# Layer 1's feed-forward: 69-column outputs for every expert, the tokens' norm on ScalarE, and a new order of the pieces

## The chip, the core and the metric

The kernel runs on one core of one Trainium2 chip. A core has TensorE (matrix multiplies; PE in the profile, its weight loads PEld), VectorE (DVE), ScalarE (ACT), GpSimd (POOL) and SyncE (SP, which only issues DMAs). Each engine works through its own list of instructions in order; semaphores tie the lists together. Matmuls write to PSUM, which this kernel uses as eight banks of 128x512 fp32. The metric is the device time of one execution in microseconds. All matrices here are fp32.

## The reference

A vision tower: 32 images of 256x256 become 256 tokens of 256 values each. Two layers follow, each with an attention and a feed-forward part. The change touches only the feed-forward part of layer 1, called stage e in the kernel:

```python
sx = jnp.einsum('bsh,ndh->bnsd', x, hl_w) + hl_b[None, :, None, :]      # 4 heads of 64
q = jnp.einsum('bnsd,neod->bneso', sx, wq)                              # 4 experts per head
k = jnp.einsum('bnsd,nod->bnso', sx, wk)
v = jnp.einsum('bnsd,nod->bnso', sx, wv)
scores = jnp.einsum('bnesd,bntd->bnest', q, k) * d ** 0.5 + causal
att = jax.nn.softmax(scores, axis=-1)
out = jnp.einsum('bnest,bntd->bnesd', att, v)                           # and laid side by side
gs = jax.nn.softmax(jnp.einsum('bnsf,nef->bnse', out, gate_w) + gate_b[None, :, None, :], axis=-1)
mixed = jnp.einsum('bnsed,bnse->bnsd', out.reshape(b, nh, s, ne, d), gs)
hn = layernorm(mixed + resid, ln_g, ln_b)                               # then fc1, relu, fc2, norm,
                                                                        # and a gate over the heads
```

Its input x is the layer norm of the tokens.

## The kernel before

Stages run one after the other: tokenizer, layer 0, layer 1's attention (stage d), and stage e from 1264 us to the end. In stage e the work of an image is cut into 59 pieces (`PIECES`), such as `(scores, 2)` or `(post, 7)`. Nothing is left to a scheduler there: `ROUND` lists pairs (back, piece), and round r does each piece for image r - back, so that nine images are in flight, from the norm of the tokens of one (back -3) to the last addition of another (back 5). When the last image's `(scores, 5)` has been issued, the rest follows a list of its own, `END`. The order of these lists is the order of each engine's instructions.

The pieces of an image, with the engine that does them:

- `tokens` normalizes the image's tokens (VectorE, line 174), `turn` transposes them on TensorE (line 750), `turned` copies them out of PSUM (ScalarE, line 1034), `heads` and `heads_out` make the heads `sx` (line 1059), of which a DMA makes a copy `sw` with the two halves of the partitions exchanged.
- `experts` multiplies `sx` with `A` (queries of all experts folded with the keys), `experts_out` copies to `g`. `head_values` multiplies with `WV`, and `head_values_out` adds `ones_row` on the way to `ev` (VectorE, line 1101).
- `scores` multiplies `sx`/`sw` with `g`, part 2 for the later keys alone. `exponentials` is ScalarE (line 1126, to `et`), and `later_keys` sets what lies above the diagonal to zero on GpSimd (line 1136).
- `outputs` multiplies `et` with columns of `ev`. For expert e these are five columns of its own (four that give the gate's logits and a one that gives the softmax's denominator) and the 64 values. As `ev` is 84 wide, [own 0, own 1, 64 values, own 2, own 3], experts 1 and 2 take 69 neighbouring columns, and experts 0 and 3 take 74, with five that nobody reads. ScalarE copies the 286 columns of all four to `eo` (line 1153).
- `post` 0 to 2 make the gate and weight the experts (VectorE, and GpSimd's multiply, line 1215), 3 adds them up, 15 and 4 square and sum, 5 scales (`er`), 6 transposes, 60 copies (`fxT`), 7 is fc1 on TensorE, 70 its relu (`hx`) and the DMAs that lay fxT and hx side by side (`both`), 8 is fc2, 80 adds (`ey`), 9 and 10 square and sum, 11 scales (`enorm`) and makes the last gate, 12, 120 and 13 transpose twice, 14 adds the tokens and stores.

TensorE runs the matmuls in three forms. Where lhsT has 128 rows and 128 columns it is one array of 128*128 (heads, fc1 and the transposes). `outputs` and fc2 have 64 columns, and two matmuls work side by side (128*64). Experts, head values and scores have 64 rows, and again two work side by side (64*128). All matmuls have line 115, that of the helper `mm`.

A tile from `bank()` is one PSUM bank, taken in turn: each must have been read by its consumer before the eighth allocation after it can be written.

Of the kernel before, what the change touches and what calls it, by code (L numbers as in the profile page):

```python
# [33 lines left out]
F32 = mybir.dt.float32  # L34
AF = mybir.ActivationFunctionType
# [44 lines left out]
def vit_tower(tc, a, out):  # L80
# [89 lines left out]
    def normed(x, b, pair):  # L170

        st, rs, i = at(pair, b)
        for c in range(NC):
            nc.vector.tensor_scalar(
                x[:, c, :], H[b][:, c, :], st[:, i, c, 0:1], rs[:, i * NC + c : i * NC + c + 1],
                ALU.subtract, ALU.mult,
            )
# [371 lines left out]

    EC = NE + 1  # L550
    VC = NE * EC + HD
    TAKE = ((0, 2 * EC + HD), (EC, EC + HD), (2 * EC, EC + HD), (2 * EC, 2 * EC + HD))
    OC = sum(w for _, w in TAKE)

    starts = [sum(w for _, w in TAKE[:e]) for e in range(NE)]
    OWN = [starts[e] + (0, EC, 2 * EC + HD, 3 * EC + HD)[e] - TAKE[e][0] for e in range(NE)]
    MIX = [starts[e] + 2 * EC - TAKE[e][0] for e in range(NE)]

# [63 lines left out]
    def prepare():  # L622
# [13 lines left out]
        for o in (NE, EC + NE, 2 * EC + HD + NE, 3 * EC + HD + NE):  # L636
            nc.gpsimd.memset(ones_row[:, o : o + 1], 1.0)
# [38 lines left out]
        for hp in range(2):  # L676
            for k, o in enumerate((0, 2 * EC + HD)):
                w = WV[:, hp, o : o + 2 * EC].rearrange("p (e x) -> p e x", e=2)
                nc.gpsimd.memset(w[:, :, NE:], 0.0)
                nc.vector.tensor_copy(  # L680
                    w[:, :, 0:NE],
                    pv[:, hp * 16 + k * 8 : hp * 16 + k * 8 + 8].rearrange("p (e x) -> p e x", e=2),
                )
# [27 lines left out]
        for hp in range(2):  # L711
            nc.vector.tensor_copy(WV[:, hp, 2 * EC : 2 * EC + HD], wv_i[:, hp, :])
# [39 lines left out]

    def normed_e(pool, b):
        x = pool.tile([P, NC, D], F32, name="ex")
        normed(x, b, st_e)
        return x

    def features(pool, x):
        xT = pool.tile([P, 2, N], F32, name="exT")
        nc.scalar.copy(xT.rearrange("p k n -> p (k n)"), feature_major(x))  # L760
        return xT
# [250 lines left out]
    with (  # L1012
# [13 lines left out]
        def tokens(b, im):  # L1026
            im.x = normed_e(p1, b)
# [70 lines left out]
        def head_values_out(b, im):  # L1098
            im.v = p2.tile([P, NC, NH, VC], F32, name="ev")
            for h, p in enumerate(im.pv):  # L1100
                nc.vector.tensor_tensor(
                    im.v.rearrange("p c (k h) x -> p (c k) h x", h=2)[:, :, h, :],
                    p[:, 0 : 2 * NC * VC].rearrange("p (g x) -> p g x", x=VC),
                    over(ones_row, [P, 2 * NC, VC], 1), ALU.add,
                )

# [34 lines left out]
        def outputs(b, im, j):  # L1141
            if j == 0:
                im.o = p2.tile([P, NC * NH, 360], F32, name="eo")
            n, c = ((0, 0), (1, 0), (0, 1), (1, 1), (2, 0), (3, 0), (2, 1), (3, 1))[j]
            p, o = bank(), 0
            for e in range(NE):
                x, w = TAKE[e]
                for m in range(c + 1):
                    t = im.t[n, e, True] if m else im.t[n, e, False][:, c * P : (c + 1) * P]
                    for q in (slice(0, HD), slice(HD, P)):  # L1150
                        mm(p[q, o : o + w], t[:, q], im.v[:, m, n, x : x + w], m == 0, m == c)
                o += w
            nc.scalar.copy(im.o[:, c * NH + n, 0:OC], p[:, 0:OC])  # L1153

# [32 lines left out]
        def expert_pair(im, k, at, w):  # L1187

            x, step = at[2 * k], at[2 * k + 1] - at[2 * k]
            return im.o[:, :, x : x + 2 * step].rearrange("p g (e x) -> p g e x", e=2)[:, :, :, 0:w]  # L1190

        def post(b, im, i):
# [102 lines left out]
            if i == 14:  # L1295
                softmax_rest(im.gate, NC)

                y = p1.tile([P, NC, D], F32, name="ex" if b > B - 6 and b % 2 else "fout")
# [16 lines left out]
            (tokens,), (turn,), (turned,), (heads,), (heads_out,), (experts, 0), (head_values,), (experts_out, 0),  # L1315
            (experts, 1), (experts_out, 1), (head_values_out,), (scores, 0), (scores, 1), (exponentials, 0),
            (exponentials, 1), (heads_zero,), (later_keys, 0), (scores, 2), (scores, 3), (scores, 4), (scores, 5),
            (exponentials, 2), (exponentials, 3), (exponentials, 4), (later_keys, 1), (exponentials, 5),
            (later_keys, 2), (later_keys, 3), (outputs, 0), (outputs, 1), (outputs, 2), (outputs, 3),
            (later_keys, 4), (outputs, 4), (outputs, 5), (later_keys, 5), (outputs, 6), (outputs, 7), (post, 0),  # L1320
            (post, 1), (post, 2), (post, 3), (post, 15), (post, 4), (post, 5), (post, 6), (post, 60), (post, 16),
            (post, 7), (post, 70), (post, 8), (post, 80), (post, 9), (post, 10), (post, 11), (post, 12), (post, 120),
# [3 lines left out]
            (1, 39), (0, 24), (0, 25), (-3, 0), (-1, 13), (4, 54), (3, 48), (4, 55), (0, 26), (0, 27), (3, 49),  # L1326
            (-1, 14), (2, 44), (2, 45), (5, 57), (1, 40), (5, 58), (-2, 3), (2, 46), (-1, 15), (-3, 1), (4, 56),
            (-2, 4), (0, 28), (0, 29), (-3, 2), (0, 30), (0, 31), (3, 50), (3, 51), (1, 41), (0, 32), (0, 33),
            (0, 34), (0, 35), (3, 52), (0, 36), (3, 53), (0, 37), (-2, 5), (-2, 6), (-1, 16), (-2, 7), (0, 38),
            (-2, 8), (-2, 9), (-1, 17), (-1, 18), (-2, 10), (1, 42), (-1, 19), (-1, 20), (2, 47), (-1, 21), (1, 43),  # L1330
            (-1, 22), (-1, 23), (-2, 11), (-2, 12),
        )
        END = (
            (3, 47), (0, 21), (0, 22), (2, 43), (5, 57), (5, 58), (0, 23), (4, 54), (2, 44), (3, 48), (3, 49),
            (0, 24), (1, 39), (0, 25), (2, 45), (2, 46), (0, 28), (0, 29), (1, 40), (0, 26), (1, 41), (2, 47),
            (0, 30), (0, 27), (0, 32), (0, 31), (0, 33), (0, 34), (1, 42), (0, 35), (0, 36), (3, 50), (1, 43),
            (3, 51), (0, 37), (3, 52), (2, 48), (2, 49), (0, 38), (0, 39), (1, 44), (1, 45), (1, 46), (4, 55),
            (0, 40), (3, 53), (4, 56), (0, 41), (3, 54), (4, 57), (2, 50), (1, 47), (2, 51), (1, 48), (1, 49),
            (0, 42), (0, 43), (4, 58), (0, 44), (3, 55), (2, 52), (2, 53), (0, 45), (3, 56), (3, 57), (3, 58),
            (0, 46), (1, 50), (0, 48), (1, 51), (0, 47), (1, 52), (0, 49), (2, 54), (2, 55), (2, 56), (2, 57),  # L1340
            (1, 53), (0, 50), (1, 54), (2, 58), (0, 51), (0, 52), (1, 55), (0, 53), (1, 56), (1, 57), (1, 58),
# [412 lines left out]
```

## Time and profile before

| | us |
|---|---|
| Median of 3 runs | 1949.14 (1946.91 to 1950.96) |
| The profiled execution | 1953.11 |
| Its span, first to last instruction | 1951.4 |
| PE busy | 1908.1 |
| DVE busy | 1209.3 |
| POOL busy | 877.5 |
| ACT busy | 821.0 |

The busy times are those of the whole program. Of stage e, 1400 to 1870 us are steady rounds of nine images; the time before that fills the pipeline, and from 1870 us on it drains. The profile's start times are those at which an instruction began on its engine. Since matmuls overlap, the distance between two starts says what one costs, rather than its length.

### The profile page before, as it was taken

Reading aid. Unit: us, or ns where it says so; the run is one execution under the profiler, and the core shown is the slowest. Engines: PE = TensorE matmul, PEld = TensorE weight load, DVE = VectorE, ACT = ScalarE, POOL = GpSimd, SP = SyncE. Lnnn points to the kernel's source line nnn. Section 1 sums busy time; section 2 is a strip of 40 time slices with the busy share of each in tenths; the row PEclk is TensorE's granted clock in tenths of the full one; section 3 lists DMA queues with packets and bytes.
Section 4 is the critical chain, followed back from the end, with each engine's and each line's share of the span. In section 5 each row is a group of like instructions: output and inputs, shape, how many; then the busy total and the mean of one; then the engine's idle time right before and its main releaser. Section 6 shows DMA issues by size and latency. Waiting matters only on the chain.

```text
span 1951.4 us, 37903 instructions
## 1 busy us (share of the span) xinstructions
PE 1908.1 (98%) x15108; PEld 1370.5 (70%) x15108; DVE 1209.3 (62%) x3225; ACT 821.0 (42%) x1549; POOL 877.5 (45%) x1072
## 2 busy tenths in 40 slices
PE   9999999999999999999989999999999999999994
PEld 7887676767676767676545555577888888888873
DVE  2334456565656574434365655545788888888886
ACT  0001222121212122212434444367878787878762
POOL 1224224343424252433443343336767676767672
PEclk9999999999999999999999999999999999999996
DMA  8540000000000042221000000011222222222212
GB/s 289 161 148 15 1 17 30 19 22 11 22 12 22 33 140 57 81 62 52 17 11 1 1 1 1 1 23 29 52 55 56 56 54 58 53 60 51 62 51 61
DMA packets 69671, 95.03 MB, mean 49 GB/s; under 512 B 8561, under 2 KB 51057, under 8 KB 69105
## 3 DMA queue, kind: packets, MB, share of 16 engines
q1 hardware_dynamic: 62768, 74.98, 13.4%
q0 software_dynamic: 6144, 16.79, 2.8%
q8 instruction: 121, 1.98, 0.4%
q10 hardware_dynamic: 576, 0.79, 0.1%
q14 instruction: 62, 0.50, 0.1%
HBM read 46.38 MB, written 20.97 MB: 35 GB/s over the span
## 4 chain that ended last, share of the span: by engine, by line
PE 95%; DVE 2%; POOL 1%; DMA 1%; ACT 0%; issue 0%; SPq 0%; ACTq 0%; DVEq 0%
PE bank L115 90%; PE bank L750 2%; PE bank L188 1%; PE bank L1294 1%; DMA patch<-in_patches_dram 0%; POOL hv L1167 0%; PE bank L229 0%; PE bank L482 0%; POOL et L1136 0%; DVE six L123 0%; DMA both<-hx 0%; POOL eo L1215 0%; DVE enorm L1273 0%; DVE ranges L1228 0%; DVE h L827 0%
## 5 line engine op out<-in xcount | busy, mean ns | idle before, releaser
L1136 POOL TENSOR_SCALAR_AFFINE_SELECT et<-et 128x256 f32<-128x256 f32 (+1 forms) x384 | 200.2, 553 | 19.4 <-ACT et L1126 18.8
L115 PE MATMUL bank<-ev,et 128*64 128x74 f32 (+1 forms) x6144 | 205.7, 227 | 1.9 <-POOL et L1136 1.9
L115 PEld LDWEIGHTS bank<-ev,et 128*64 128x64 f32 x6144 | 197.6, 138 | 8.0 <-issue 5.2
L1126 ACT ACTIVATE et<-bank 128x512 f32<-128x512 f32 x384 | 201.0, 660 | 0.0
L115 PE MATMUL bank<-tokW,patch 128*128 128x256 f32 x768 | 169.1, 383 | 2.7 <-DMA patch<-in_patches_dram 2.7
L115 PE MATMUL bank<-g,sx 64*128 64x512 f32 (+1 forms) x512 | 170.7, 483 | 0.0
L115 PE MATMUL bank<-g,sw 64*128 64x512 f32 (+1 forms) x512 | 170.3, 483 | 0.0
L115 PEld LDWEIGHTS bank<-tokW,patch 128*128 128x128 f32 x768 | 147.7, 193 | 24.4 <-issue 3.5
L1153 ACT COPY eo<-bank 128x286 f32<-128x286 f32 x256 | 101.9, 402 | 91.1 <-PE bank L115 78.7
L115 PE MATMUL bank<-bxT,w_wuv 128*128 128x512 f32 x300 | 131.4, 592 | 0.0
L115 PEld LDWEIGHTS bank<-g,sw 64*128 64x128 f32 x512 | 95.7, 187 | 33.0 <-issue 21.9
L148 POOL TENSOR_SCALAR rs_c<-st_c 128x4 f32<-128x4 f32 x16 | 3.1, 191 | 251.8 <-DVE st_c L124 251.8
L1215 POOL TENSOR_TENSOR eo<-eo,gate 128x1024 f32<-128x1024 f32 x60 | 115.2, 1940 | 1.5 <-DVE gate L1212 1.5
L115 PE MATMUL bank<-wvo,dm 128*128 128x512 f32 x256 | 114.3, 599 | 0.0
L115 PE MATMUL bank<-attn,bv 128*128 128x256 f32 x512 | 113.1, 379 | 0.0
L115 PE MATMUL bank<-w_wo,gT 128*128 128x256 f32 x512 | 113.1, 379 | 0.0
L115 PE MATMUL bank<-w_w,hT 128*128 128x256 f32 x512 | 113.1, 379 | 0.0
L115 PE MATMUL bank<-xsel,w_w 128*128 128x512 f32 x256 | 111.4, 592 | 0.0
L1167 POOL TENSOR_TENSOR hv<-hv,minus_half 128x8 f32<-128x8 f32 x64 | 108.8, 1699 | 5.3
L115 PEld LDWEIGHTS bank<-attn,bv 128*128 128x128 f32 x512 | 97.2, 190 | 19.6 <-issue 6.9
L115 PEld LDWEIGHTS bank<-g,sx 64*128 64x128 f32 x512 | 95.7, 187 | 19.4 <-issue 14.8
L123 DVE BATCH_NORM_STATS2 six<-h 128x6 f32<-128x256 f32 x256 | 105.6, 412 | 4.4
(268 smaller groups left out, 3845.6 us busy)
## 6 DMA issues: line engine op xcount, KB each, us to landing
patch<-in_patches_dram SPq DMA_DIRECT2D x31, 768.0 KB, 4.6
sw<-sx SPq DMA_DIRECT2D x64, 128.0 KB, 2.7
both<-fxT SPq DMA_DIRECT2D x64, 128.0 KB, 3.2
both<-hx SPq DMA_DIRECT2D x64, 128.0 KB, 2.4
out_dram<-fout SPq DMA_DIRECT2D x29, 256.0 KB, 2.1
cs<-ranked SPq DMA_DIRECT2D x32, 128.0 KB, 2.0
results<-cy SPq DMA_DIRECT2D x32, 128.0 KB, 1.7
w_w<-in_w_dram SPq DMA_DIRECT2D x2, 1024.0 KB
```

The costliest lines, as they stand in the source:

```text
L115: nc.tensor.matmul(o, lhsT, rhs, start=first, stop=last)
L123: nc.vector.bn_stats(six, x)
L148: nc.gpsimd.tensor_scalar(o, var, 1.0, 1e-5, ALU.mult, ALU.add)
L188: nc.tensor.transpose(p[:, o : o + P], x[:, c, k * P : (k + 1) * P], ident)
L750: nc.tensor.transpose(p[:, o : o + P], x[:, c, k * P : (k + 1) * P], ident)
L1126: nc.scalar.activation(t, p, AF.Exp)
L1136: nc.gpsimd.affine_select(out=own, in_=own, pattern=[[0, n_e], [1, P]], compare_op=ALU.is_ge, fill=0.0, base=0, channel_multiplier=-1,)
L1153: nc.scalar.copy(im.o[:, c * NH + n, 0:OC], p[:, 0:OC])
L1167: nc.gpsimd.tensor_tensor(v, v, minus_half, ALU.pow)
L1215: (nc.vector if b > B - 3 else nc.gpsimd).tensor_tensor(im.mix[k], im.mix[k], over(im.gate[:, :, 2 * k : 2 * k + 2], [P, NC * NH, 2, HD], ...
L1294: nc.tensor.transpose(im.po[:, o : o + P], im.fT[:, k, c * P : (c + 1) * P], ident)
```

## The change

1. `ev` becomes 148 wide: [own 0, 64 values, own 1, own 2, 64 values again, own 3]. Every expert's five columns now lie beside a copy of the values, so each takes 69 columns, from 0, 5, 74 and 79, and `eo` is 276 wide instead of 286. `WV` stays 84 wide, in the order own 0, values, own 1, own 2, own 3. `head_values_out` now writes each half of the heads with three VectorE additions (74 columns, 5 and 5) and one ScalarE copy of the 64, so that there are six and two per image instead of two and none.
2. `tokens` moves from VectorE to ScalarE: an activation with scale and bias per token. The bias, minus mean times scale, is one 128x2 operation on VectorE.
3. `PIECES`, `ROUND` and `END` are ordered anew. On TensorE a round was: post 7, 12, 6 and 13, heads, turn; outputs 0 to 3, post 8, outputs 4 to 7; experts 0, head values, experts 1, scores 2 to 5, 0 and 1. It is now: heads, post 12, 13 and 6; outputs 0 to 3, post 8, outputs 4 to 7; turn; experts 0; post 7; scores 2 to 5, head values, experts 1, scores 0 and 1. On GpSimd `later_keys` 4 and 5 now stand ahead of the multiply of post 2, and 1 to 3 behind it, mixed with the powers of post 10 and 4. Image 31's end list moves too: post 0 and 1 of image 30 and fc1 of image 28 stand ahead of the last scores.
4. The last stores of images 27, 29 and 31 use the buffer of `exT` instead of `ex`.

The diff; of the three lists the old lines are left out:

```diff
--- before.py
+++ after.py
@@ -547,14 +547,16 @@
     LOW, HIGH = 1e-28, 1e28
 
 
     EC = NE + 1
+    WC = EC + HD
     VC = NE * EC + HD
-    TAKE = ((0, 2 * EC + HD), (EC, EC + HD), (2 * EC, EC + HD), (2 * EC, 2 * EC + HD))
-    OC = sum(w for _, w in TAKE)
-
-    starts = [sum(w for _, w in TAKE[:e]) for e in range(NE)]
-    OWN = [starts[e] + (0, EC, 2 * EC + HD, 3 * EC + HD)[e] - TAKE[e][0] for e in range(NE)]
-    MIX = [starts[e] + 2 * EC - TAKE[e][0] for e in range(NE)]
+    VU = 2 * (WC + EC)
+    TAKE = (0, EC, WC + EC, WC + 2 * EC)
+    OC = NE * WC
+    OWN = [e * WC + (0, HD)[e % 2] for e in range(NE)]
+    MIX = [e * WC + (EC, 0)[e % 2] for e in range(NE)]
 
     right_e, right_d, passing = ExitStack(), ExitStack(), ExitStack()
     pwe = right_e.enter_context(tc.tile_pool(name="e_w", bufs=1, side="right", reuse_waits="tile"))
@@ -633,7 +635,7 @@
         ones_d = pm.tile([P, P], F32, name="ones_d")
         nc.gpsimd.memset(ones_d, 1.0)
         nc.gpsimd.memset(ones_row, 0.0)
-        for o in (NE, EC + NE, 2 * EC + HD + NE, 3 * EC + HD + NE):
+        for o in (NE, WC + NE, WC + EC + NE, WC + 2 * EC + NE):
             nc.gpsimd.memset(ones_row[:, o : o + 1], 1.0)
         gfg = pm.tile([P, 2, NH], F32, name="gfg")
         nc.vector.tensor_scalar(gfg, fg, col("fn_g"), None, ALU.mult)
@@ -674,13 +676,10 @@
 
         nc.scalar.mul(A.rearrange("p h x -> p (h x)"), pa, math.sqrt(HD))
         for hp in range(2):
-            for k, o in enumerate((0, 2 * EC + HD)):
-                w = WV[:, hp, o : o + 2 * EC].rearrange("p (e x) -> p e x", e=2)
-                nc.gpsimd.memset(w[:, :, NE:], 0.0)
-                nc.vector.tensor_copy(
-                    w[:, :, 0:NE],
-                    pv[:, hp * 16 + k * 8 : hp * 16 + k * 8 + 8].rearrange("p (e x) -> p e x", e=2),
-                )
+            for e, o in enumerate((0, WC, WC + EC, WC + 2 * EC)):
+                w = WV[:, hp, o : o + EC]
+                nc.gpsimd.memset(w[:, NE:], 0.0)
+                nc.vector.tensor_copy(w[:, 0:NE], pv[:, hp * 16 + e * NE : hp * 16 + (e + 1) * NE])
 
         p = bank()
         mm(p[:, 0 : 2 * NH], cen, gfg.rearrange("p k x -> p (k x)"))
@@ -709,7 +708,7 @@
         centred(f2.unsqueeze(1), f2.unsqueeze(1), 1)
         centred(wv_i, wv_i, 2)
         for hp in range(2):
-            nc.vector.tensor_copy(WV[:, hp, 2 * EC : 2 * EC + HD], wv_i[:, hp, :])
+            nc.vector.tensor_copy(WV[:, hp, EC:WC], wv_i[:, hp, :])
 
         yield
         for i in range(2):
@@ -749,16 +748,6 @@
                 o = k * N + c * P
                 nc.tensor.transpose(p[:, o : o + P], x[:, c, k * P : (k + 1) * P], ident)
         return p
-
-    def normed_e(pool, b):
-        x = pool.tile([P, NC, D], F32, name="ex")
-        normed(x, b, st_e)
-        return x
-
-    def features(pool, x):
-        xT = pool.tile([P, 2, N], F32, name="exT")
-        nc.scalar.copy(xT.rearrange("p k n -> p (k n)"), feature_major(x))
-        return xT
 
 
     class Pair:
@@ -1024,7 +1013,15 @@
         halves = [slice(h * HD, (h + 1) * HD) for h in range(2)]
 
         def tokens(b, im):
-            im.x = normed_e(p1, b)
+            im.x = p1.tile([P, NC, D], F32, name="ex")
+            st, rs, i = at(st_e, b)
+            rs = rs[:, i * NC : (i + 1) * NC]
+            less = spool.tile([P, NC], F32, name="e_less")
+            nc.vector.scalar_tensor_tensor(less, st[:, i, :, 0], -1.0, rs, ALU.mult, ALU.mult)
+            for c in range(NC):
+                nc.scalar.activation(
+                    im.x[:, c, :], H[b][:, c, :], AF.Identity, bias=less[:, c : c + 1], scale=rs[:, c : c + 1]
+                )
 
         def turn(b, im):
             im.pt = feature_major(im.x)
@@ -1096,13 +1093,22 @@
                         mm(p[:, o : o + VC], im.sx[s, hp, c * P : (c + 1) * P], WV[s, hp, :])
 
         def head_values_out(b, im):
-            im.v = p2.tile([P, NC, NH, VC], F32, name="ev")
+            im.v = p2.tile([P, NC, NH, VU], F32, name="ev")
             for h, p in enumerate(im.pv):
+                v = im.v.rearrange("p c (k h) x -> p (c k) h x", h=2)[:, :, h, :]
+                p = p[:, 0 : 2 * NC * VC].rearrange("p (g x) -> p g x", x=VC)
+                first = WC + EC
                 nc.vector.tensor_tensor(
-                    im.v.rearrange("p c (k h) x -> p (c k) h x", h=2)[:, :, h, :],
-                    p[:, 0 : 2 * NC * VC].rearrange("p (g x) -> p g x", x=VC),
-                    over(ones_row, [P, 2 * NC, VC], 1), ALU.add,
+                    v[:, :, 0:first], p[:, :, 0:first], over(ones_row[:, 0:first], [P, 2 * NC, first], 1), ALU.add
                 )
+                nc.vector.tensor_tensor(
+                    v[:, :, first : first + EC], p[:, :, first : first + EC],
+                    over(ones_row[:, first : first + EC], [P, 2 * NC, EC], 1), ALU.add,
+                )
+                nc.vector.tensor_tensor(
+                    v[:, :, VU - EC :], p[:, :, first + EC :], over(ones_row[:, first + EC :], [P, 2 * NC, EC], 1), ALU.add
+                )
+                nc.scalar.copy(v[:, :, first + EC : VU - EC], p[:, :, EC:WC])
 
         def scores(b, im, k):
 
@@ -1140,17 +1146,18 @@
 
         def outputs(b, im, j):
             if j == 0:
-                im.o = p2.tile([P, NC * NH, 360], F32, name="eo")
+                im.o = p2.tile([P, NC * NH * OC + MIX[2]], F32, name="eo")
             n, c = ((0, 0), (1, 0), (0, 1), (1, 1), (2, 0), (3, 0), (2, 1), (3, 1))[j]
             p, o = bank(), 0
             for e in range(NE):
-                x, w = TAKE[e]
+                x, w = TAKE[e], WC
                 for m in range(c + 1):
                     t = im.t[n, e, True] if m else im.t[n, e, False][:, c * P : (c + 1) * P]
                     for q in (slice(0, HD), slice(HD, P)):
                         mm(p[q, o : o + w], t[:, q], im.v[:, m, n, x : x + w], m == 0, m == c)
                 o += w
-            nc.scalar.copy(im.o[:, c * NH + n, 0:OC], p[:, 0:OC])
+            o = (c * NH + n) * OC
+            nc.scalar.copy(im.o[:, o : o + OC], p[:, 0:OC])
 
         def in_range(b, first, n):
             return ranges[:, b // 8 % 2, b % 8, first : first + n]
@@ -1187,7 +1194,8 @@
         def expert_pair(im, k, at, w):
 
             x, step = at[2 * k], at[2 * k + 1] - at[2 * k]
-            return im.o[:, :, x : x + 2 * step].rearrange("p g (e x) -> p g e x", e=2)[:, :, :, 0:w]
+            rows = im.o[:, x : x + NC * NH * OC].rearrange("p (g x) -> p g x", x=OC)
+            return rows[:, :, 0 : 2 * step].rearrange("p g (e x) -> p g e x", e=2)[:, :, :, 0:w]
 
         def post(b, im, i):
             if i == 0:
@@ -1295,7 +1303,7 @@
             if i == 14:
                 softmax_rest(im.gate, NC)
 
-                y = p1.tile([P, NC, D], F32, name="ex" if b > B - 6 and b % 2 else "fout")
+                y = p1.tile([P, NC, D], F32, name="exT" if b > B - 6 and b % 2 else "fout")
                 y8 = y.rearrange("p c (n d) -> p (c n) d", d=HD)
                 nc.vector.tensor_tensor(
                     y8, im.po.rearrange("p (g d) -> p g d", d=HD),
@@ -1312,33 +1320,32 @@
 
         images = [Image() for _ in range(B)]
         PIECES = (
...
+            (tokens,), (turn,), (turned,), (heads,), (heads_out,), (experts, 0), (experts_out, 0), (head_values,),
+            (head_values_out,), (experts, 1), (experts_out, 1), (scores, 0), (scores, 1), (exponentials, 0),
+            (exponentials, 1), (later_keys, 0), (later_keys, 1), (scores, 2), (scores, 3), (exponentials, 2),
+            (exponentials, 3), (later_keys, 2), (heads_zero,), (scores, 4), (exponentials, 4), (later_keys, 3),
+            (scores, 5), (exponentials, 5), (later_keys, 4), (later_keys, 5), (outputs, 0), (outputs, 1),
+            (outputs, 2), (outputs, 3), (outputs, 4), (outputs, 5), (outputs, 6), (outputs, 7), (post, 0), (post, 1),
+            (post, 2), (post, 3), (post, 15), (post, 4), (post, 5), (post, 6), (post, 60), (post, 7), (post, 16),
+            (post, 70), (post, 8), (post, 80), (post, 9), (post, 10), (post, 11), (post, 12), (post, 120),
             (post, 13), (post, 14),
         )
         ROUND = (
...
+            (0, 28), (0, 29), (-1, 13), (-2, 3), (2, 44), (4, 54), (4, 55), (-1, 14), (5, 57), (2, 45), (-2, 4),
+            (-1, 15), (0, 30), (4, 56), (1, 40), (2, 46), (0, 31), (-3, 0), (0, 32), (0, 33), (5, 58), (3, 50),
+            (0, 34), (3, 51), (0, 35), (-1, 16), (3, 52), (1, 41), (0, 36), (0, 37), (-3, 1), (-2, 5), (3, 53),
+            (-3, 2), (-2, 6), (2, 47), (1, 42), (-1, 17), (-1, 18), (2, 48), (2, 49), (-1, 19), (-1, 20), (0, 38),
+            (0, 39), (-1, 21), (-1, 22), (-1, 23), (-1, 24), (1, 43), (-1, 25), (-1, 26), (-1, 27), (-2, 7), (-2, 8),
+            (-2, 9), (-2, 10), (-2, 11), (-2, 12),
         )
         END = (
...
+            (0, 28), (0, 27), (0, 30), (5, 57), (5, 58), (1, 40), (2, 44), (0, 31), (0, 32), (2, 45), (2, 46),
+            (3, 50), (4, 54), (1, 41), (1, 42), (0, 29), (2, 47), (0, 33), (2, 48), (2, 49), (1, 43), (0, 34),
+            (4, 55), (4, 56), (3, 51), (3, 52), (3, 53), (1, 44), (0, 35), (0, 36), (0, 37), (0, 38), (0, 39),
+            (1, 45), (1, 46), (2, 50), (0, 40), (0, 41), (1, 47), (1, 49), (1, 48), (0, 42), (0, 43), (3, 54),
+            (2, 51), (4, 57), (0, 44), (0, 45), (2, 52), (1, 50), (3, 55), (2, 53), (4, 58), (1, 51), (0, 46),
+            (0, 47), (1, 52), (1, 53), (3, 56), (0, 49), (3, 57), (2, 54), (2, 55), (2, 56), (2, 57), (3, 58),
+            (0, 48), (1, 54), (0, 50), (1, 55), (2, 58), (0, 51), (0, 52), (0, 53), (1, 56), (1, 57), (1, 58),
             (0, 54), (0, 55), (0, 56), (0, 57), (0, 58),
         )
         LAST = PIECES.index((scores, 5))
```

## The prediction

> **What bounds the kernel now.** First the table of stretches, for the stage that the change touches (from 1264 us on):
>
> ```profile
> core 0: us, PE busy (x) PEld busy (x) DVE busy (x) ACT busy (x) POOL busy (x), PEclk, DMA share, GB/s
> 1500.00:1600.00 100.00, 100.00 (x1588) 81.39 (x1586) 85.25 (x203) 80.05 (x175) 69.23 (x93) 1.00 0.22 55
> 1870.00:1951.40 81.40, 51.04 (x682) 38.36 (x679) 60.42 (x158) 33.74 (x71) 35.06 (x45) 0.77 0.20 54
> ```
>
> TensorE has no idle time in the steady rounds; only the tail from 1870 us, at a lower clock, waits. "Busy" counts overlapped latencies, though, so next I read the starts in TensorE's timeline, one round of the loop (start, length of the group, group):
>
> ```profile
> 1600.79 0.59 PE L115 MATMUL bank<-g,sx 64*128 64x512 f32 x1
> 1601.21 0.59 PE L115 MATMUL bank<-g,sw 64*128 64x512 f32 x1
> 1601.22 0.59 PE L115 MATMUL bank<-g,sx 64*128 64x512 f32 x1
> 1601.74 1.13 PE L115 MATMUL bank<-fxT,w_fc 128*128 128x512 f32 x2
> 1602.70 0.60 PE L750 MATMUL bank<-ident,enorm 128*128 128x128 f32 x4
> ...
> 1605.74 0.60 PE L750 MATMUL bank<-ident,ex 128*128 128x128 f32 x4
> 1606.27 3.20 PE L115 MATMUL bank<-ev,et 128*64 128x74 f32 x96
> 1609.30 1.12 PE L115 MATMUL bank<-W,both 128*64 128x68 f32 x32
> 1610.25 3.15 PE L115 MATMUL bank<-ev,et 128*64 128x74 f32 x96
> 1613.33 1.14 PE L115 MATMUL bank<-sx,A 64*128 64x256 f32 x8
> ...
> 1621.31 1.12 PE L115 MATMUL bank<-fxT,w_fc 128*128 128x512 f32 x2
> ```
>
> The round is 1621.31 - 1601.74 = 19.57 us. The form before each size is rows*columns of the array in use. A pair of 64*128 matmuls of 512 columns takes 0.43 us (1600.79 to 1601.22), but the step to the first 128*128 matmul is 0.52, 0.09 too much, and in single records the second w_fc matmul follows 0.533 us after the first where 512 columns need 0.427: 0.106 more. The same two excesses stand wherever the form changes, always alike: 64*128 to 128*128 0.092+0.106; 128*128 to 128*64 0.096+0.053; 128*64 to 64*128 0.095+0.107; 128*128 to 64*128 (layer 1's attention and the first rounds) 0.095+0.107; 128*64 to 128*128 0.096+0.106. So no semaphore causes them; a change of form costs 0.15 to 0.20 us. A round before has three: 0.55 us.
>
> [...]
>
> **The change part by part.**
>
> ```profile
> L1153 ACT COPY eo<-bank 128x286 f32<-128x286 f32 x144 | 57.3, 398 | 47.8 <-PE bank L115 40.2
> L1059 ACT ACTIVATE sx<-bank,cols 128x256 f32<-128x256 f32 x36 | 17.6, 620 | 0.0
> L1238 ACT ACTIVATE fxT<-bank,cols 128x512 f32<-128x512 f32 x18 | 16.3, 907 | 0.0
> L1101 DVE TENSOR_TENSOR ev<-bank,ones_row 128x336 f32<-128x336 f32 x34 | 15.6, 501 | 4.4 <-PE bank L115 4.4
> L174 DVE TENSOR_SCALAR ex<-h,st_e,rs_e 128x256 f32<-128x256 f32 x36 | 13.1, 406 | 0.0
> 1325.33 3.04 ACT L1126 ACTIVATE et<-bank 128x512 f32<-128x512 f32 x6
> ```
>
> *Outputs all 69 wide.* In single starts sixteen 74-wide matmuls take 0.513 us, sixteen 69-wide 0.480; over all stretches 32.0 and 30.1 ns each. Half of an image's 192 narrow: 96 x 1.9 ns = -0.18 us, on the path. For 31 images before the tail: -5.6 us.
>
> *Places anew, on TensorE.* The order of a round is now heads, three transposes (128*128); outputs and fc2 (128*64); the token transpose `turn` (128*128); experts 0 (64*128); fc1, post 7 (128*128); scores 2 to 5, head values, experts 1, scores 0 and 1 (64*128). Six changes of form instead of three: `turn` and fc1 used to stand in one run of 128*128 and are now islands. Added are one 128*64 to 128*128 (0.135: [...] between 0.10 and 0.20), one 64*128 to 128*128 (0.198) and one 128*128 to 64*128, with the 128*64 to 64*128 replaced by an equal one: +0.53. Round: 19.57 + 0.53 - 0.18 = 19.92. Counted in the program's order up to the last image's scores: 96 changes before (17.6 us at these prices), 182 after (32.9 us): +15.2.
>
> *Norm of tokens on ScalarE.* VectorE loses 2 x 406 ns and gains one 128x2 operation (about 0.17). ScalarE gains two of 256 with two per-partition operands: [...]. Hidden in the steady round under TensorE: `turn` needs them only 3 us later. In the first two rounds nothing hides them: `turn` waits for heads_out and then 1.15 us of norm. Before, sx of image 0 ended at 1278.21 while `turn` began at 1278.00; now about 1279.2: +1.2. A round later it ends at 1286.63, so `turn` at 1287.6 and experts 0.58 behind, against 1286.32: +1.9. Together +3.1.
>
> *Values 148 wide.* VectorE: two operations of 336 become two of 296 and four of 20 (0.46 and about 0.17 each; they start some 0.08 before the predecessor ends): +0.5 us; with the norm about zero. ScalarE: two copies of 256 from PSUM, 0.37 (the 286 row less 30 elements), back to back 0.28. ScalarE's round: before 14.3 us at back-to-back pace (the exponentials 12 x 0.476: six take 3.04), after 14.3 + 0.9 + 0.56 - 0.07 = 15.7 of 19.9.
>
> I walked one round in the new order with these durations, heads at 0: outputs 3.2 to 10.0, `turn` 10.1, experts 10.7, fc1 11.7, scores 2 to 5 from 12.8 to 16.3, head values to 17.15, experts 1 to 18.06, scores 0 and 1 to 19.8. Margins before TensorE would wait (8 banks, each taken 8 allocations later): enorm for post 12 is ready at 0.7, wanted at 1.8; bank of outputs 4 wants VectorE's fout, which the POOL multiply ahead of it holds (as at 1604.09, 1.94 us), at 5.8, wanted 7.1; tokens 6.8, wanted 10.1; bank of scores 0 wants the exponentials of scores 4 at 17.0, wanted 18.06; scores 1 those of scores 5 at 17.95, wanted 18.9. All hidden, with 1 us to spare. POOL's order leaves the selects done well before each output.
>
> *Fill and last full round.* Before, TensorE stood 2.6 us in the outputs at 1332 (the selects sat behind POOL's multiplies), 0.4 at 1328 and 1.35 at 1881: 4.3. The selects now stand ahead of the multiplies: these go, the 3.1 above come: -1.2. fc1 of image 28 is done before the tail: +1.0 there.
>
> *Tail.* Before: last score matmul 1889.73, end 1951.4: 61.7 us, a serial chain over the last image with its neighbours' work ahead of it in each queue (outputs done at +15.4, er x rs +31.3, fc2 +41.2, last enorm +50.1, last add ends +55.5, then 6.2). Walked through the new end order with the tail's own durations (VectorE 0.69 per 512, POOL power 1.65 + 0.2, reshuffle 3.0): TensorE waits from +3 to +7 for image 29's er behind the multiplies of image 30; outputs done +14.8, er x rs +28.0, fc2 +39.3, enorm +47.1, add ends +52.5: 58.7, so -3.0, good to 4 us either way.
>
> Sum: +15.2 - 5.6 + 1.0 - 1.2 - 3.0 = **+6.4 us**. The profiled execution took 1953.11 us, 1.7 of it outside its span of 1951.4; it would have a span of 1957.8. The median of the runs is 1949.14, so 1955.5.
>
> **Rivals.** (A) A wait enters each round: ScalarE. An exponential pair takes 0.95 us where a score pair takes 0.85, so ScalarE falls behind in the scores; hx or the gate's exponential 1 us later than walked makes scores 0 wait one for one. For it: ScalarE rises from 73 to 79%. Against: the margins. At 0.3 us in 28 rounds: +8.4, 1964. (B) Fill and tail win more than walked, 7 us instead of 3 and the 3.1 at the start half hidden: 1950, not to be told from before. (C) Faster: the changes of form cost nothing where a semaphore or a load would have held TensorE anyway. Without the 15.2 the sum is -8.8: 1940. 86 more changes decide it at 8.8/86 = 0.10 us each: below that it is faster. Against: the trace shows 0.15 to 0.20 at each one in steady work, in five kinds. (D) The narrowing does nothing because a 64-column load sets the pace: +12, 1961; against, 69 wide is faster than 74 in each stretch, and 68 (29.6 ns) faster still.
>
> **Numbers.** Forecast with or without D 0.58, A 0.17, B 0.17, C 0.08. Single runs of before spread 4 us, and 0.2% (3.9 us) is about what a measurement of this kernel can tell from no change. Range 1950 to 1966: it leaves out C, the better half of B, and an A of over 0.4 us a round. Slower over 0.2%: most of the forecast and A, 0.74; within 0.2%: 0.18; faster: 0.08.
>
> **What would show it.** Right: a steady round of 19.9 us, [...] 69-wide outputs at 30.1 ns; some 1 us before `turn` in the first two rounds; no bubble near 1332. Wrong: a round under 19.6, a steady wait of TensorE on ScalarE, VectorE or POOL, or a tail off 59 us by over 5.

## The result, and the profile after

The changed kernel takes 1966.03 us (median, 1962.50 to 1969.29) against 1950.05 (1946.91 to 1951.98) for the kernel before, measured beside it: a ratio of 1.0083, 95% interval 1.0056 to 1.0110. It is slower by 16 us; the forecast was 6.4 slower. Repeated later it took 1965.96 and 1967.22 (ratios 1.0082 and 1.0087). The profiled execution took 1969.29 us with a span of 1966.6, 15.2 us over the span before. The remaining 0.8 to 1 us isn't in the span: each execution of the changed kernel takes 2.7 to 3.2 us more than its span from first to last instruction, each of the kernel before 1.6 to 1.8 us.

The table of stretches of the kernel after (columns as before):

```profile
core 0: us, PE busy (x) PEld busy (x) DVE busy (x) ACT busy (x) POOL busy (x), PEclk, DMA share, GB/s
1500.00:1600.00 100.00, 100.00 (x1590) 78.84 (x1586) 82.89 (x213) 86.01 (x192) 71.88 (x91) 1.00 0.23 56
1870.00:1966.60 96.60, 63.76 (x992) 49.33 (x988) 77.07 (x198) 46.31 (x101) 47.29 (x55) 0.86 0.21 54
```

In the steady rounds TensorE still has no idle time, at the full clock (PEclk, the granted share of TensorE's clock, is 1.00). ScalarE rose from 80 to 86 and VectorE fell from 85 to 83: neither is the bound. So what grew there is TensorE's own round. One round in TensorE's timeline after (start, length, group):

```profile
1614.12 0.59 PE L115 MATMUL bank<-g,sx 64*128 64x512 f32 x1
1614.64 1.99 PE L115 MATMUL bank<-exT,w_hl 128*128 128x256 f32 x8
...
1617.35 0.60 PE L749 MATMUL bank<-ident,er 128*128 128x128 f32 x4
1617.88 3.11 PE L115 MATMUL bank<-ev,et 128*64 128x69 f32 x96
1620.81 1.12 PE L115 MATMUL bank<-W,both 128*64 128x68 f32 x32
1621.76 3.06 PE L115 MATMUL bank<-ev,et 128*64 128x69 f32 x96
1624.75 0.66 PE L749 MATMUL bank<-ident,ex 128*128 128x128 f32 x4
1625.34 1.13 PE L115 MATMUL bank<-sx,A 64*128 64x256 f32 x8
1626.40 1.12 PE L115 MATMUL bank<-fxT,w_fc 128*128 128x512 f32 x2
1627.46 0.48 PE L115 MATMUL bank<-g,sx 64*128 64x256 f32 x1
...
1634.58 1.99 PE L115 MATMUL bank<-exT,w_hl 128*128 128x256 f32 x8
```

From heads to heads are 19.94 us, and 19.93 on the mean of 24 rounds. `turn` at 1624.75 and fc1 at 1626.40 each stand alone between groups of another form. The step from turn to experts 0 is 0.59 us where four transposes inside a run of their form take 0.44; experts 0 takes 1.06 instead of the 0.97 of before, and fc1 1.06 instead of 0.96.

The groups of ScalarE and VectorE after, 1400 to 1752 us (busy, mean ns, idle before):

```profile
L1160 ACT COPY eo<-bank 128x276 f32<-128x276 f32 x143 | 54.2, 396 | 26.0 <-PE bank L115 23.6
L1022 ACT ACTIVATE ex<-h,e_less,rs_e 128x256 f32<-128x256 f32 x36 | 20.2, 624 | 0.0
L1111 ACT COPY ev<-bank 128x256 f32<-128x256 f32 x34 | 12.8, 376 | 3.2 <-DVE ev L1108 2.8
...
L1101 DVE TENSOR_TENSOR ev<-bank,ones_row 128x296 f32<-128x296 f32 x35 | 16.1, 461 | 51.7 <-PE bank L115 51.7
L1104 DVE TENSOR_TENSOR ev<-bank,ones_row 128x20 f32<-128x20 f32 x34 | 5.7, 167 | 0.0
L1020 DVE SCALAR_TENSOR_TENSOR e_less<-st_e,rs_e 128x2 f32<-128x2 f32 x17 | 2.6, 153 | 0.0
```

The added operations last about what the prediction took for them: 0.38, 0.46, 0.17 and 0.15 us where 0.37, 0.46, 0.17 and about 0.17 stood. An activation of the norm takes 0.62 us, and the pair 1.09 where my estimate was 1.15.

I cut stage e by the starts of groups on TensorE. "Fill" runs from the first transpose of image 0's tokens to the heads of round 0, the third heads; "end" from the heads of round 29, the last image's, to the start of the last score matmul; "tail" from there to the end of the span. r0, r5 and r29 are the starts of rounds 0, 5 and 29. Times are from the profiles, in us; the last three rows are experiments described below.

| | fill | r0 to r5 | r5 to r29 (one round) | end | tail | stage e |
|---|---|---|---|---|---|---|
| before | 20.3 | 94.4 | 469.7 (19.57) | 31.0 | 62.0 | 677.4 |
| after | 29.3 | 92.3 | 478.3 (19.93) | 32.6 | 60.3 | 692.8 |
| after, 2nd profile | 28.1 | 92.3 | 478.3 (19.93) | 32.6 | 61.6 | 692.8 |
| after, 3rd profile | 28.0 | 92.3 | 478.3 (19.93) | 32.6 | 59.9 | 691.1 |
| tokens first | 21.9 | 92.3 | 478.4 (19.93) | 32.6 | 61.3 | 686.3 |
| three forms, tokens first | 21.9 | 90.6 | 465.4 (19.39) | 31.4 | 63.3 | 672.5 |
| places without wide values | 24.7 | 92.9 | 482.8 (20.12) | 32.9 | 60.7 | 694.0 |

Steady rounds (+8.7) and fill (+7.7 to +9.0) carry the loss. The first rounds in the timeline, before, with line 174 VectorE's norm of the tokens:

```profile
1274.65 0.41 DVE L174 TENSOR_SCALAR ex<-h,st_e,rs_e 128x256 f32<-128x256 f32 x1
...
1278.00 0.61 PE L750 MATMUL bank<-ident,ex 128*128 128x128 f32 x4
1278.54 1.14 PE L115 MATMUL bank<-sx,A 64*128 64x256 f32 x8
```

The same in the timeline after (in brackets: idle time before, and what ended it):

```profile
1276.10 1.66 DVE L944 SCALAR_TENSOR_TENSOR h<-bank,d_rs,h 128x256 f32<-128x256 f32 x4 [1.41 <-POOL d_rs L149]
...
1276.95 1.00 PE L115 MATMUL bank<-w_hl,exT 128*128 128x64 f32 x8
1277.15 0.84 ACT L1056 ACTIVATE sx<-bank,cols 128x256 f32<-128x256 f32 x2 [2.08 <-PE bank L115]
...
1278.54 0.27 DVE L1046 TENSOR_TENSOR res<-bank,rows_e 128x128 f32<-128x128 f32 x1
...
1279.13 0.14 DVE L1020 SCALAR_TENSOR_TENSOR e_less<-st_e,rs_e 128x2 f32<-128x2 f32 x1
...
1279.36 1.09 ACT L1022 ACTIVATE ex<-h,e_less,rs_e 128x256 f32<-128x256 f32 x2 [1.37 <-DVE e_less L1020]
...
1280.02 1.39 PE L749 MATMUL bank<-ident,ex 128*128 128x128 f32 x4 [2.07 <-ACT ex L1022]
1281.34 2.08 PE L115 MATMUL bank<-sx,A 64*128 64x256 f32 x8
```

Two things are to be seen. TensorE stood for 2.07 us before `turn`. ScalarE was done with the heads (`sx`) at 1278.0, and its norm then waited 1.37 us for the tokens' bias `e_less`. That stood late in VectorE's list, behind the attention's last additions `h`, statistics of other tokens and `res` (the residual, from the heads' second matmuls); from 1276.10 to `e_less` VectorE had no idle time. Before, the norm stood early in the round, ahead of those additions, and was done at 1275.5. The second wait, 1.27 us a round later, has another cause: there the bias is in time, and the norm starts right behind an exponentials' table load (1.28), four exponentials and `sx` in ScalarE's own list.

Then, `turn` and experts 0 take about twice their time (2.08 where 1.14 was): the clock went to half rate. In the table of stretches PEclk is 0.52 for these 7 us:

```profile
1280.00:1287.00 7.00, 6.97 (x38) 5.49 (x40) 1.18 (x6) 3.02 (x7) 1.20 (x2) 0.52 0.06 12
```

By its clock record after has two such stretches here, 6.83 us from 1279.8 and 3.41 us from 1293.5 (PEclk 0.50 in both); before has none from 993 us to 1893 (PEclk 1.00).

### The profile page after: what moved, and what is told of

Read it like the earlier page. It is cut to its first block, busy times and chain, and to the rows that moved or that the text cites. A ratio compares the mean times of both kernels' runs of the same rounds, so it can differ in the third digit from the quotient of the medians.

```text
span 1966.6 us, 38148 instructions
## 1 busy us (share of the span) xinstructions
PE 1919.8 (98%) x15108; PEld 1361.9 (69%) x15108; DVE 1206.0 (61%) x3325; ACT 871.2 (44%) x1677; POOL 890.8 (45%) x1076
## 4 chain that ended last, share of the span: by engine, by line
PE 94%; DVE 4%; DMA 1%; ACT 1%; issue 0%; POOL 0%; ACTq 0%; DVEq 0%
PE bank L115 89%; PE bank L749 2%; PE bank L188 1%; PE bank L1302 1%; DMA patch<-in_patches_dram 0%; PE bank L229 0%; PE bank L482 0%; DVE eo L1223 0%; DVE six L123 0%; DVE six L934 0%; DVE fout L1312 0%; DVE h L816 0%; DMA tokW<-in_tokW_dram 0%; DVE fout L1308 0%; DVE enorm L1281 0%
## 5 line engine op out<-in xcount | busy, mean ns | idle before, releaser
L1142 POOL TENSOR_SCALAR_AFFINE_SELECT et<-et 128x256 f32<-128x256 f32 (+1 forms) x384 | 214.5, 591 | 78.1 <-ACT et L1132 77.1
L115 PE MATMUL bank<-ev,et 128*64 128x69 f32 x6144 | 197.2, 223 | 0.0
L115 PEld LDWEIGHTS bank<-ev,et 128*64 128x64 f32 x6144 | 189.7, 136 | 6.3 <-issue 5.7
L115 PE MATMUL bank<-g,sx 64*128 64x512 f32 (+1 forms) x512 | 179.9, 490 | 0.0
L115 PE MATMUL bank<-g,sw 64*128 64x512 f32 (+1 forms) x512 | 178.5, 491 | 0.0
L1160 ACT COPY eo<-bank 128x276 f32<-128x276 f32 x256 | 96.5, 397 | 48.2 <-PE bank L115 43.9
```

The lines of the kernel that those rows point to most:

```text
L115: nc.tensor.matmul(o, lhsT, rhs, start=first, stop=last)
L1142: nc.gpsimd.affine_select(out=own, in_=own, pattern=[[0, n_e], [1, P]], compare_op=ALU.is_ge, fill=0.0, base=0, channel_multiplier=-1,)
L1160: nc.scalar.copy(im.o[:, o : o + OC], p[:, 0:OC])
```

## The experiments

All keep the computation of the kernel whole. The theory after seeing the result: the steady rounds cost what was forecast, and the rest is the fill, waits and clock together. Rivals: the wide values' extra work on VectorE and ScalarE; the norm's engine rather than its place.

**Tokens first.** The changed kernel, with the tokens' norm at the head of the round:

```diff
         ROUND = (
-            (0, 28), (0, 29), (-1, 13), (-2, 3), (2, 44), ...
-            ... (0, 31), (-3, 0), (0, 32), ...
+            (-3, 0), (0, 28), (0, 29), (-1, 13), (-2, 3), (2, 44), ...
+            ... (0, 31), (0, 32), ...
```

> The kernel after, with the piece tokens moved to the head of each round, so that the 128x2 operation stands ahead of the residual's addition on VectorE and the norm ahead of heads_out on ScalarE. If the first rounds lost their 9 us because turn waited for the norm (2.2 us and 1.3 us) [...], both go: heads of image 2 start some 7 us earlier (near 1296 us instead of 1303.2), steady round unchanged at 19.93, time 1959 (9 above before). Rival: the loss sits in the new places of experts and head values, and the norm is innocent: 1966, heads of image 2 still near 1303.

Measured: 1959.88 us (1956.34 to 1964.16), ratio 1.0049 (1.0031 to 1.0067). The fill fell by 7.4 us to 21.9, without half rate (experts 0 take 1.13 us), and the steady round is unchanged. So the place of `tokens` costs about 6 us of the 16. It leaves 1.6 us over before in the fill; in that timeline:

```profile
1285.01 1.13 PE L115 MATMUL bank<-sx,A 64*128 64x256 f32 x8 [1.59 <-ACT sx L1056]
```

Experts 0 of image 1 wait for `sx`, which ScalarE makes after the norm, a table load (1.28) and four exponentials.

**Filler.** The changed kernel, and TensorE does eight 128x128 matmuls that nobody reads while it waits, ahead of `turn` of images 1 and 2:

```diff
         def turn(b, im):
+            if b in (1, 2):
+                p = bank()
+                for _ in range(8):
+                    mm(p[:, 0:128], ident, ident)
             im.pt = feature_major(im.x)
```

> The kernel after, with eight matmuls of 128x128 that nobody reads ahead of turn of images 1 and 2 (1.7 us each at full rate), so that TensorE does work while it waits for the norm. If the waits alone cost the time: no change or up to 0.5 us slower, 1966. If the idle time brings the half-rate clock, and that is most of the loss: no half-rate window between 1270 and 1300 us and some 5 us faster, 1961, with the waits for the norm still there.

Measured: 1963.26 us (1960.82 to 1966.81), ratio 1.0069 (1.0054 to 1.0084). No half rate in the fill (PEclk 1.00 from 1263 to 1300 us), which took 25.4 us, although the norm is as late as ever: `turn` of image 1 starts 3.07 us behind the heads' second matmuls in both kernels, and the filler takes 2.00 of it. It lies between the two expectations, and of the 2.8 us won against the changed kernel some 1.1 lie outside the span, where this kernel takes 1.7 us like the kernel before. The profile has 3.9 us less of fill than the 29.3, but a later experiment has the same waits without half rate and without filler (PEclk 1.00), so this one alone would not have settled it.

**Three forms.** Tokens first, and `turn` and fc1 go back into one run of 128*128 with heads and transposes (fc1 one round later):

```diff
-            (0, 28), (0, 29), (-1, 13), (-2, 3), (2, 44), ... (2, 45), (-2, 4),
-            ... (0, 31), (-3, 0), (0, 32), ... (0, 37), (-3, 1), (-2, 5), (3, 53),
-            (-3, 2), (-2, 6), (2, 47), (1, 42), ... (2, 48), (2, 49), (-1, 19), ...
+            (-3, 0), (0, 28), (0, 29), (-1, 13), (3, 47), (3, 49), (-2, 3), (2, 44), ... (2, 45), (-3, 1), (-2, 4),
+            ... (0, 31), (-3, 2), (0, 32), ... (0, 37), (-2, 5), (3, 53),
+            (-2, 6), (1, 42), ... (2, 48), (-1, 19), ...
         END = (
-            (0, 28), (0, 27), ...
+            (3, 47), (3, 49), (0, 28), (0, 27), ...
```

> As e1, and turn and fc1 (post 7, with post 70) put back into the run of 128*128 matmuls around the heads: three changes of form a round instead of six. If changes of form make the steady round: 19.93 - 0.53 = 19.4 us and, with e1's fill, 1944 (6 under before). Rival: the round of 19.93 comes from ScalarE's or VectorE's added work, which is all still here: 19.9 and 1959.

Measured: 1944.91 us (1943.70 to 1948.47), ratio 0.9970 (0.9959 to 0.9980), faster than both kernels. The round is 19.39 us. Its timeline:

```profile
1599.53 0.59 PE L115 MATMUL bank<-fxT,w_fc 128*128 128x512 f32 x1
1599.96 1.89 PE L115 MATMUL bank<-exT,w_hl 128*128 128x256 f32 x8
1601.69 0.60 PE L749 MATMUL bank<-ident,enorm 128*128 128x128 f32 x4
...
1603.00 0.60 PE L749 MATMUL bank<-ident,ex 128*128 128x128 f32 x4
1603.53 3.11 PE L115 MATMUL bank<-ev,et 128*64 128x69 f32 x96
```

The round has three changes of form (two expectations below call them four). Heads take 1.73 from start to start instead of 1.83, the transposes 0.44, and 19.93 - 19.39 = 0.54 us a round is what three more changes of form cost. Step by step, all of it lies where the form changes: 0.15 us at `turn` (0.135 by my estimate) and 0.09 to 0.11 each at experts 0, fc1, the first scores behind it and heads; every other step of the two rounds is equal. They cost time, whatever the reason for their place. (Of the 15 us won over tokens first, about 1 lies outside the span.)

**Wide values alone.** The kernel before with part 1 (and the buffers of part 4), in the old order and with VectorE's norm.

> The kernel before with part 1 of the change alone: values 148 wide, all outputs 69 columns, three VectorE additions and a ScalarE copy per half; norm on VectorE and the old places. If 1.9 ns for each of 96 matmuls an image is right and the added VectorE and ScalarE work is hidden: round 19.57 - 0.18 = 19.39, time 1944.5 (5.6 under before). Rival (a 64-column weight load sets the pace, or VectorE's four more operations delay others): 19.57 or more, 1950 or more.

Measured: 1961.45 us (1959.91 to 1964.29), ratio 1.0055 (1.0040 to 1.0070). I had expected the narrowing's gain and it is a loss: the round is 19.85 us, where 19.39 was expected and 19.57 was before. The narrowing is there (outputs 2.94 and 2.99 us for 96), but the scores take 5.41 instead of 5.26, and post 12's transposes 0.74 instead of 0.44. In its timeline, with ScalarE and TensorE's weight loads:

```profile
1601.36 0.67 ACT L1104 COPY ev<-bank 128x256 f32<-128x256 f32 x2
...
1602.42 3.07 ACT L1125 ACTIVATE et<-bank 128x512 f32<-128x512 f32 x6
...
1606.15 0.14 PEld L749 LDWEIGHTS bank<-ident,enorm 128*128 128x128 f32 x1 [0.24 <-ACT et L1125]
...
1607.29 0.42 PEld L749 LDWEIGHTS bank<-ident,er 128*128 128x128 f32 x4 [0.35 <-ACT et L1125]
```

The bank that a transpose takes must have been read by the exponentials, and they stand behind the two new copies.

**Wide values, copies on VectorE.** The same, with one line changed:

```diff
-                nc.scalar.copy(v[:, :, first + EC : VU - EC], p[:, :, EC:WC])
+                nc.vector.tensor_copy(v[:, :, first + EC : VU - EC], p[:, :, EC:WC])
```

> The kernel with the wide values alone (part 1 in the old order, round 19.85 us, 1961), but the two copies of the 64 values are on VectorE instead of ScalarE. Theory: it was ScalarE's two copies, which stand ahead of the exponentials in its list, that made TensorE wait in the scores (5.41 instead of 5.26 us) and before the transposes of post 12 (0.75 instead of 0.44 us). Then the scores go back to 5.26, the round to about 19.4 to 19.5, and the time to 1945 to 1948. Rival: VectorE's longer work in head_values_out is what is late (its next consumers wait); then the copies on VectorE make it worse, with a round of 19.9 or more and a time over 1962.

Measured: 1947.42 us (1944.72 to 1950.03), ratio 0.9985 (0.9978 to 0.9993). The scores are back at 5.26, post 12's transposes at 0.44 in most rounds (0.52 on the mean), the fill at 20.3 and the round at 19.47. Its timeline:

```profile
1610.47 3.04 ACT L1125 ACTIVATE et<-bank 128x512 f32<-128x512 f32 x6
...
1615.01 0.60 PE L749 MATMUL bank<-ident,enorm 128*128 128x128 f32 x4
...
1615.44 0.60 PE L749 MATMUL bank<-ident,er 128*128 128x128 f32 x4
```

So ScalarE's two copies, 0.67 us ahead of its exponentials, made the old order wait, not VectorE's work. With one line moved, part 1 alone is a gain.

**Norm on ScalarE alone.** The kernel before with part 2 only; `tokens` keeps its old place, fourth in the round.

> The kernel before with the tokens' norm on ScalarE alone (part 2), in the old order. My theory now says that the first two rounds of the new kernel lose 9 us because the small bias operation stands late in VectorE's list; here it stands early, so it isn't late. What is left is the wait for ScalarE: the prediction put it at +3.1 us, one expectation then is a fill longer by 3 us, a steady round of 19.57 us as before, and 1953. If the wait is hidden here, as in the kernel with the wide values alone (fill +0.5), the time is that of before, 1950. If ScalarE's 0.9 us more in a round aren't hidden in the old order, the steady round grows to 19.7 or more and the time passes 1955.

Measured: 1954.26 us (1950.59 to 1959.77), ratio 1.0018 (1.0009 to 1.0026). The round is 19.57 and the fill 21.2 us: the engine costs 0.9 us, not 3, and no round. Stage e took 678.5 us, 1.1 over before. The rest of the 3.6 us lies, in these two profiles, ahead of stage e, where nothing was changed: the stage begins 2.7 us later. Why, no run shows.

**Places without wide values.** The changed kernel, with values and outputs as before (part 1 undone).

> The changed kernel without its first part: new places and norm on ScalarE, but values 84 wide and outputs of 74 and 69 columns as before. By the prediction's term for the narrowing (96 matmuls of 192 by 1.9 ns, 0.18 us an image) the steady round is 20.11 us instead of 19.93 and the time 5.6 us above that of the changed kernel: 1971.6. If the narrowing does nothing on the path (rival D), round and time stay at 19.93 and 1966. If the extra operations of the wide values cost something in the new places as they did in the old, the round falls below 19.93 and the time below 1966.

Measured: 1968.58 us (1965.59 to 1971.24), ratio 1.0089 (1.0076 to 1.0102). The round is 20.12 us, as expected: the narrowing is worth 0.19 us a round on the path, and rival D falls. But the time is only some 1 us above the changed kernel by the ratios, and not 5.6, since the fill took 24.7 us instead of 29.3. Its timeline shows the same waits, and its table of stretches then the full clock:

```profile
1279.23 0.33 PE L750 MATMUL bank<-ident,ex 128*128 128x128 f32 x1 [2.07 <-ACT ex L1033]
...
1280.20 1.13 PE L115 MATMUL bank<-sx,A 64*128 64x256 f32 x8
...
1288.83 0.33 PE L750 MATMUL bank<-ident,ex 128*128 128x128 f32 x1 [1.27 <-ACT ex L1033]
...
1280.00:1287.00 7.00, 7.00 (x56) 5.22 (x54) 0.92 (x2) 5.51 (x10) 1.31 (x3) 1.00 0.00 1
```

This sets the waits alone: 24.7 - 20.3 = 4.4 us.

**The changed kernel twice more.** No edit.

> The changed kernel once more, unchanged, for its clock in the first rounds. In its first profile the fill took 29.3 us with 10.2 us at half rate; two kernels with the same waits had none and filled in 24.7 and 25.4. If half rate follows from those waits each time, this profile has it too and the runs lie together near 1968. If it comes in some executions alone, the runs fall into two groups, near 1962.5 with a mean granted clock of 0.992 and near 1969 with 0.988 to 0.989, and a profile without it fills in 25 us.

> The changed kernel a third time, with the same expectations as the second.

Measured: 1965.96 us (1963.26 to 1970.79) and 1967.22 us (1963.88 to 1969.64). Both profiles have half rate in the fill, two stretches of about 3.4 us each (the first of the two: PEclk 0.57 from 1280 to 1284 us and 0.59 from 1290 to 1294; the other: `experts` 1 of image 0 takes 1.99 us and experts 0 of image 1 takes 2.08, where places alone had 1.07 and 1.13), and fills of 28.1 and 28.0 us: 3.4 us more than with the waits alone, half of the 6.8 us. The first profile had 10.2 us and lost 4.6. So all three profiles of this kernel have it, in two lengths; the runs spread over 1962 to 1971 without a clear gap, which settles neither expectation for the other executions.

**Norm of the first four images on VectorE.** Added to the three-forms version:

```diff
         def tokens(b, im):
             im.x = p1.tile([P, NC, D], F32, name="ex")
+            if b < 4:
+                normed(im.x, b, st_e)
+                return
```

> The version with tokens first and four changes of form a round (1944.9), but the norm of the first four images' tokens is on VectorE, as before. If what the fill still loses against the kernel before (22.0 instead of 20.3 us) is ScalarE's list in the first rounds (the second heads_out behind norm and exponentials), the fill is back to 20.3 to 20.8 and the time at 1943.5. If it's the order of the other pieces, the fill stays at 22 and the time at 1945.

Measured: 1945.80 us (1943.69 to 1949.32), ratio 0.9973 (0.9963 to 0.9984). The fill fell to 20.9 us and the wait for `sx` from 1.6 to 0.6, nearly what was expected; but the stage as a whole took 672.3 us against 672.5, as end and tail took 0.6 us more. In time it can't be told from the version without.

**The old end list.** On top of that, `END` in the order of the kernel before, less the nine pieces that the new round has already done.

> The version with tokens first, four changes of form a round and the first norms on VectorE (1945.8), with the end list in the order of the kernel before (less the nine pieces that the new round has already done). From the heads of the last round but two to the end of the span the kernel before takes 93.0 us and this version 95.3. If the order of the end list is what costs the 2.3 us, they go and the time is 1943.5; if it's the state in which the new round hands over (what is still to do at the last scores), the time stays at 1945.8.

Measured: 1945.63 us (1943.07 to 1948.38), ratio 0.9975 (0.9967 to 0.9983). From the last heads to the end are 95.9 us, not less. So the old order of the list doesn't bring the 2.3 us back. By the expectation that leaves what the round hands over, but no run changes that alone.

## Why the prediction was right and wrong

The direction and the steady round were right, the size was not: 16 us slower where 6.4 stood. Term by term, in the first profile's times:

| term of the forecast | forecast | measured |
|---|---|---|
| steady rounds r5 to r29: 24 x (0.53 - 0.18) | +8.4 | +8.7 |
| r0 to r5: bubbles gone, fewer added changes as fc1 starts in r3 | -2.4 | -2.2 |
| fill: norm on ScalarE | +3.1 | +9.0 |
| end: two rounds, fc1 of image 28, bubble of 1881 gone | +0.4 | +1.6 |
| tail | -3.0 | -1.7 |
| sum | +6.5 | +15.4 |

(The forecast's terms are split here by stage, and rounded; its sum was 6.4. The spans differ by 15.2, since stage e began 0.2 us earlier after. What lies outside the span comes on top; the forecast took it as 1.7 us, as before.)

**Changes of form and narrowing** held in each part: 19.93 against 19.92, 0.54 against 0.53 by the three-forms version, 0.19 against 0.18 by the places without wide values. Rival C, that the changes cost nothing, and D fall. Rival A, a wait of ScalarE in every round, doesn't occur in the new places; in the old ones it does (wide values alone), so ScalarE's margin is a matter of the order, as the walk said.

**The step that failed** is "In the first two rounds nothing hides them ... Together +3.1". The place of the wait was right, before `turn` of images 1 and 2. It was sized by ScalarE's norm alone: `turn` of image 1 was put at 1279.2 and came at 1280.0. ScalarE was free when I had reckoned, at 1278.0, and with my estimate of 1.15 us for the norm (measured 1.09) 1279.2 would have held; but the bias came 1.37 us later, since it stood late in VectorE's list. I counted what stands ahead on the engine that does the norm, and not on the one that makes its operand. The waits are 4.4 us, 1.3 more. And the cause was the new place more than the engine, whose own part is 0.9 (norm on ScalarE alone).

The larger part was not in the sum at all: the clock. The three profiles lose 3.3 to 4.6 us to half rate after these waits, by my estimate from their fills of 28.0 to 29.3 us and the 24.7 of the waits alone. Nothing in the prediction asked what the clock does behind TensorE's waits, though the lines it showed had a PEclk of 0.77 in a tail where TensorE is busy for 51.04 of 81.40 us.

**Tail and end** together are 2.5 us worse than forecast. The tail is 60.3, 61.6 and 59.9 us in three profiles (before 62.0), inside the 4 us that were allowed. In the end the wait of fc2 for `hx` shrank from 1.35 to 0.35 us instead of going, and scores 0 and 1 took 2.02 instead of 1.81.

**Outside the span.** The forecast carried over the 1.7 us of before. In the three measurements of the changed kernel, and with tokens first and places without wide values, it is 2.4 to 3.3 us in every execution; in the kernel before and the other experiments, the filler and the three forms among them, 1.6 to 1.8. The traces of before and after put it at the end: the last semaphore update comes 2.9 us after the last instruction in after, and 1.9 in before. So about 1 us of the 16 is no part of stage e. What causes it no run shows.

## What to carry to other kernels

Count TensorE's changes of form per round when pieces are moved: three were worth 0.54 us a round, more than the narrowing gave, and regrouping them made the same change a gain. A piece's place binds on each engine that it uses: follow the operand's producer through its own list, down to an operation of 0.15 us; here that list cost more than the operation. Where a wait is added on TensorE, price the clock after it too (3.3 to 4.6 us here, behind waits of 4.4), and where work is moved to an engine ask what it now stands ahead of.

## What the runs showed of the hardware

*Half rate stood behind waits of 2.07 and 1.27 us.* In the clock records of the profiles of before and after, the half-rate stretches in stage e last 3.41, 6.83 or 10.24 us, but for the last, which the end cuts, and within each profile they start whole multiples of 3.41 us apart. For the 3.41 us ahead of each, the tables of stretches of these two profiles give:

| profile | half rate from, us | TensorE busy in the 3.41 us ahead, us |
|---|---|---|
| after, fill | 1279.8, 1293.5 | 1.52, 1.99 |
| after, tail | 1914.7, 1931.8, 1952.3 | 0.00, 0.36, 0.16 |
| before, tail | 1893.7, 1910.8, 1917.6, 1931.3, 1938.1 | 0.93, 1.50, 1.17, 1.49, 0.66 |

Such a stretch doesn't bring half rate each time: the 3.41 us from 1907.9 of after have 1.63 us of busy time, and the next 3.41 us are at PEclk 1.00. "Places without wide values" had the same waits of 2.07 and 1.27 us and, from 1263 to 1300 us, TensorE busy for 32.66 us of 37, at PEclk 1.00; after has 32.82 us there, at 0.86. So neither the length of the waits nor their sum sets the clock alone, and why this run escaped was not shown.

*The filler* kept the clock: from 1263 to 1300 us TensorE is busy for 35.71 us of 37, at PEclk 1.00. The price is work that nobody reads: a fill of 25.4 us, where the waits alone take 24.7 and waits with half rate 28.0 to 29.3.
